# Attention: joining of blocks in four parts, scalings over three steps, z turned behind the fourth transposes, late matmuls of odd steps in the products' bank

## The chip, the cores and the metric

The kernel runs on one core of one Trainium2 chip. The time is the device time of that core in microseconds, the median of three runs. The engines of a core work in parallel, each through its own queue of instructions in program order, and wait for each other by semaphores: TensorE (PE; its weight loads are PEld), VectorE (DVE), ScalarE (ACT), GpSimd (POOL) and SyncE (SP, which issues the DMAs).

## The reference

The program is one layer of three parts, in 32-bit floats:

```
x = x + cross_attention(layernorm(x), ctx)      # x: 16 x 128 x 512, ctx: 16 x 2048 x 512, 16 heads of 32
x = x + mamba_and_mlp(layernorm(x))             # selective scan over 128 steps, then a gelu MLP with two rmsnorms
x = x + mixture_ffn(layernorm(x))               # shared and expert product, two best of 7 gates
```

What the change touches is the attention:

```
attn = softmax(q @ k.T * scale)                 # over 2048 context rows, for each head
out  = (attn @ v) reshaped to 128 x 512
x    = x + out @ wo.T + bo
```

The kernel takes the 2048 context rows in four blocks of 512, each with its own maximum and its own sum of exponentials. The four blocks of a head are joined afterwards: with m the maximum over the blocks, each block's product is multiplied by exp(m_block - m) over the sum of (block sum x exp(m_block - m)).

## The kernel before

The first phase is one long loop over steps u = 0 to 255 (`live`), step u = 16 b + 4 sb + hg: batch b of 16, context block sb of 4, group hg of four heads. A tail of steps up to 313 runs the rest of the scans, interleaved with the MLP and the last part. Each step is written out by hand, and each engine runs it in the order of the code. TensorE, in a live step: the scores of four heads (`scores`, line 299, into the four PSUM banks `bank0` to `bank3`), the product of the step before with v (`weighted`, L343, into `avp`), the first half of a Strassen-like product that makes k and v of the next block (`x_products`, L237, in the PSUM tiles `pa` and `pc`), the transposes of the exponentials (`turn`, L330: four groups of four, group i in a bank), the "late" matmuls, and the second half of the products (`y_products`, L237). One step of two has one product in that second half (odd u, `pa` only), the other has two (even u, `pc` and `pa`).

VectorE takes the maxima of the four banks (L307), ScalarE the exponentials (L317) and copies of transposed banks (L335); one of the four is copied by VectorE (L333). From step 54 on, the scans of the second part run beside this (LAG = 22 steps behind the end of a pair of batches): in every step ScalarE makes decays (L656), VectorE two scans (L670) and products (L673), GpSimd the inputs (L635) and the running sums (L682, L686); every fourth step (u = 1 mod 4) GpSimd ends a group with L689, L690 and L691. GpSimd also makes the sums t of context tiles (L229) in these steps.

The work that comes once per batch is put into tables by step: `loads` (at the step's start), `head` (ahead of the maxima), `middle` and `late` (behind the third or fourth group of transposes; `late` functions get a bank), `behind` (behind the late ones, into `pc`), `after`, and `inner` (at the end, ahead of `y_products`' sums). With e = 16 (b + 1), the step behind the batch's last, these are:

- `joined`, `shares`, `joined_second`, `joined_third`: the joining factors (L418 four copies that gather the maxima, L423 their least negative, L424 the differences, L428 the exponential on ScalarE, L432 to L434 the sum and its reciprocal, L439 the factors).
- `spread_out` (L445, GpSimd, spreads a block's factors over 512 columns in a tile `fx`) and `scaled` (four transposes L451 of `fx`, and VectorE's multiply, L456 for block 0 and L458 for the others; for these GpSimd adds the result into `aT`, L459).
- `attended` in step e+6: the output projection (`out_proj`, L464) of `aT`, and the addition to x.
- `normed` and `z_turned` (L511, copy L513): the layernorm of the second part and its transposes, in steps e+7 and e+8.
- For the next batch: `load_x`, `moments_of`, `root_of`, `normal` (L373, and L376 on GpSimd), `turned` (L385, copied by L387) and `queries` (L395).

A step with late work does three groups of transposes, then the late matmuls in banks 3, 0, 1 and so on, and then the fourth group in the next bank. A bank can be used again when the copy or multiply that reads it is done; the scores of the next step need all four.

Of the kernel before, what the change touches and what calls it, by code (L numbers as in the profile page):

```python
# [34 lines left out]
def perceiver_layer(ctx: ExitStack, tc: tile.TileContext, a: dict, out: bass.AP):  # L35
# [73 lines left out]
    with ExitStack() as es:  # L109
# [251 lines left out]
        def moments_of(b):  # L361
            moments(keep, mv[:, b, :], xts[b])
            xts[b, "r"] = root_first(keep, mv[:, b, 1:2], 1e-5)

        def root_of(b):
            root_second(*xts[b, "r"])
# [15 lines left out]
        def turned(b, ps):  # L382
            xn = xts.pop((b, "n"))
            for kc in range(KC):
                nc.tensor.transpose(heads(ps)[:, kc, :], xn[:, kc * P : (kc + 1) * P], ident)  # L385
            xnT = keep.tile([P, KC, P], FP, tag="fx", name="xnT")
            nc.vector.tensor_copy(xnT, heads(ps))  # L387
            xts[b, "t"] = xnT
# [24 lines left out]
        def joined(b):  # L413

            parts, sm = stats[b]
            nm = keep.tile([P, SB, H], FP, tag="nm", name=f"nm{b}")
            for j in range(4):
                nc.vector.tensor_copy(  # L418
                    nm.rearrange("p s (k j) -> p s k j", j=4)[:, :, :, j], parts[j]
                )  # L420
            lo = keep.tile([P, 1, H], FP, tag="lo", name="lo")
            flat = lo.rearrange("p a h -> p (a h)")
            nc.vector.tensor_reduce(flat, nm.rearrange("p s h -> p h s"), AX.X, ALU.min)  # L423
            nc.vector.tensor_tensor(nm, lo.to_broadcast([P, SB, H]), nm, ALU.subtract)  # L424
            stats[b] = nm, sm, lo, flat

        def shares(b):
            nc.scalar.activation(stats[b][0], stats[b][0], AF.Exp)  # L428
# [322 lines left out]
        def bank():  # L751
            return free_banks.pop(0)
# [316 lines left out]


        late, after, inner, middle, loads, head, behind = ({} for _ in range(7))

        def put(where, u, f):
            where.setdefault(u, []).append(f)

        for b in range(B):
            s = 16 * b
            if b:
                put(loads, s - 8, lambda b=b: load_x(b))
                put(loads, s - 5, lambda b=b: load_w(0, b))  # L1080
                put(inner, s - 7, lambda b=b: moments_of(b))
                put(middle, s - 6, lambda b=b: root_of(b))
                put(inner, s - 6, lambda b=b: normal(b))
                put(late, s - 5, lambda ps, b=b: turned(b, ps))
                put(late, s - 4, lambda ps, b=b: queries(b, ps))
            e = s + 16
            put(loads, e + 5, lambda b=b: load_w(3, b))
            put(inner, e - 1, lambda b=b: joined(b))
            put(middle, e, lambda b=b: shares(b))
            put(head, e + 1, lambda b=b: joined_second(b))  # L1090
            put(head, e + 2, lambda b=b: joined_third(b))
            for sb in range(SB):
                put(inner, e + 2 + sb // 2, lambda b=b, sb=sb: spread_out(b, sb))
                put(late, e + 3 + sb // 2, lambda ps, b=b, sb=sb: scaled(b, sb, ps))
            put(late, e + 6, lambda ps, b=b: attended(b, ps))
            put(middle, e + 7, lambda b=b: root_of(b))
            put(inner, e + 7, lambda b=b: normed(b))
            put(late, e + 8, lambda ps, b=b: z_turned(b, ps))
        for g in range(NG):
            p = 32 * (g + 1)  # L1100
            for ec in range(EC):
                put(loads, p + 8 + ec, lambda g=g, ec=ec: load_win(g, ec))
                put(loads, p + 8 + ec, lambda g=g, ec=ec: load_win(g, EC + ec))
                put(late, p + 9 + ec, lambda ps, g=g, ec=ec: x_part(g, ec, ps))
                put(late, p + 9 + ec, lambda ps, g=g, ec=ec: z_part(g, ec, ps))
                put(after, p + 10 + ec, lambda g=g, ec=ec: silu_first(g, ec, xas))
                put(after, p + Z_GATES[ec], lambda g=g, ec=ec: silu_first(g, ec, zss))
            put(late, p + 18, lambda ps, g=g: x_proj(g, ps))
            s = p + LAG
            for ec in range(EC):  # L1110
                put(loads, s - 4 + 4 * ec, lambda ec=ec: load_dtproj(ec))
                put(behind, s - 3 + 4 * ec, lambda ps, g=g, ec=ec: dt_first(g, ec, ps))
                put(middle, s - 2 + 4 * ec, lambda g=g, ec=ec: dt_second(g, ec))
                put(inner, s - 2 + 4 * ec, lambda g=g, ec=ec: dt_third(g, ec))
            for i in range(GB):
                for ec in range(WS):
                    put(loads, s + 32 + 2 * i, lambda g=g, i=i, ec=ec: load_wout(g, i, ec))
                put(loads, s + 31 + 2 * i, lambda b=g * GB + i: reload_x(b))
                put(late, s + 33 + 2 * i, lambda ps, g=g, i=i: projected(g, i, ps))
# [46 lines left out]
        for u in range(last):  # L1166
            live = u < NU
            g, r = divmod(u - 32 - LAG, 32)
            scans = 0 <= g < NG

            made, phase = divmod(u + 3, 4)
            makes = 0 < made < B * SB
            of, phase = ("k", "v")[phase // 2], phase % 2
            load_bc(u + 2 - 32 - LAG, 0)
            if u % 4 == 1 and made + 1 < B * SB:
                load_ctx(made + 1, ("c00", "c10", "c11"))
            if u % 4 == 2 and made + 1 < B * SB:
                load_ctx(made + 1, ("c01",))
            for f in loads.get(u, ()):
                f()  # L1180
            if scans:
                decays(g, r, 0)
            if u > NU:
                while fed < feeds * (u - NU) // (last - 1 - NU):
                    feed(fed)
                    fed += 1
            load_bc(u + 1 - 32 - LAG, DS)
            if u == NU + 1:
                load_rows()
            if live:  # L1190
                scores(u)
            if 1 <= u <= NU:
                weighted(u - 1)
            if u == NU:
                att.close()
                give_back(flat(pa), banks[2], banks[1], flat(avp))
                open_ffn()
            if u == NU + 8:
                load_wex()
            for f in head.get(u, ()):  # L1200
                f()
            if live:
                maxima(u)
            if makes:
                x_products(of, made, phase, pa, pc)
            if live:
                exps(u)
            if makes and u % 4 == 1:
                ctx_sums(made, ("t1", "t2"))
            if 0 <= u + 1 - 32 - LAG < 32 * NG:  # L1210
                inputs(*divmod(u + 1 - 32 - LAG, 32))
            if makes and u % 4 == 1:
                ctx_sums(made, ("t3", "t4"))
            silu_third()
            if scans:
                scan(g, r, 0)
            if makes:
                hold(of, made, pa, "u1")
            if scans:
                decays(g, r, 1)  # L1220
            if makes:
                x_sums(of, made, phase, pa, pc)


            after_turns = late.get(u, ())
            if live:
                for i in range(3 if after_turns else 4):
                    turn(u, i, i)
            if scans:
                scan(g, r, 1)  # L1230
            for f in middle.get(u, ()):
                f()
            for i, f in enumerate(after_turns):
                ps = banks[(3 + i) % 4] if live else bank()
                f(ps)
                if not live:
                    give_back(ps)
            if live and after_turns:
                turn(u, 3, (3 + len(after_turns)) % 4)
            for f in behind.get(u, ()):  # L1240
                ps = flat(pc) if makes else banks[2] if live else bank()
                f(ps)
                if not live:
                    give_back(ps)
            for f in after.get(u, ()):
                f()
            for f in inner.get(u, ()):
                f()
            if makes:
                y_products(of, made, phase, pa, pc)  # L1250
                y_sums(of, made, phase, pa, pc)
            silu_second()
# [76 lines left out]
```

## Time and profile before

| what | us |
|---|---|
| median of 3 runs (3818.95 to 3823.20) | 3820.44 |
| the profiled execution, its own time | 3821.1 |
| its span in the trace | 3819.3 |
| steps u = 0 to 255 begin and end at about | 57.6 and 3126 |
| TensorE busy in the span | 3747.7 |
| VectorE busy | 2711.8 |
| ScalarE busy | 2445.3 |
| GpSimd busy | 2104.1 |

The span is the time from the first to the last instruction of the program in the trace. Rows of a group give the line, engine, operation, tiles and shapes, the count, the busy time, the mean duration and the idle time of the engine in front. Rows in order of time give the start, the duration and what is merged in them; times such as "+5.64" in the text are counted from the start of the step's first score matmul. The granted TensorE clock is 0.993 of full.

### The profile page before, as it was taken

The page shows a single profiled execution, that of the slowest core. Times are in us where ns is not written, and L with a number is a line of the kernel's source. Part 1 is how long each engine was busy: PE and PEld are TensorE (multiplying, and loading weights), DVE is VectorE, ACT ScalarE, POOL GpSimd, SP SyncE. Part 2 cuts the span into 40 slices and gives each one's busy share as a digit, 9 for nine tenths or more (in the row PEclk, how much of TensorE's full clock was granted, in tenths as well). Part 3 has the DMA queues.
Part 4 walks back from the last instruction along what each step waited for, and adds up shares of the span by engine and source line. Part 5 has one row for each costly group of instructions (what it writes and reads, how often), then busy time and mean ns, then how long its engine had stood idle before and what let it go on. Part 6 is the DMA issues. An engine that isn't in the chain of part 4 may idle for free.

```text
span 3819.3 us, 70341 instructions
## 1 busy us (share of the span) xinstructions
PE 3747.7 (98%) x26120; PEld 2856.3 (75%) x26120; DVE 2711.8 (71%) x4852; ACT 2445.3 (64%) x5847; POOL 2104.1 (55%) x1968
## 2 busy tenths in 40 slices
PE   7999999999999999999999999999999989999999
PEld 6878787778777877788778877787878766656555
DVE  3444444887878787878788778877887777677843
ACT  3555556777767776777677767776777665545421
POOL 1111113676657666765666666666675667567730
PEclk9999999999999999999999999999999999999999
DMA  3111122444353435343534453445444447577752
GB/s 92 39 38 42 45 75 65 145 141 155 121 172 133 158 119 182 130 155 115 188 125 147 129 191 123 145 131 179 135 157 131 158 169 272 193 263 257 264 191 72
DMA packets 341223, 548.40 MB, mean 144 GB/s; under 512 B 24432, under 2 KB 225408, under 8 KB 340624
## 3 DMA queue, kind: packets, MB, share of 16 engines
q1 hardware_dynamic: 340464, 543.28, 42.9%
q8 instruction: 206, 3.38, 0.3%
q14 instruction: 137, 1.12, 0.1%
q0 software_dynamic: 416, 0.63, 0.1%
HBM read 527.29 MB, written 16.52 MB: 142 GB/s over the span
## 4 chain that ended last, share of the span: by engine, by line
PE 84%; DVE 9%; ACT 3%; issue 2%; DMA 1%; POOL 1%; SPq 0%; DVEq 0%; ACTq 0%; POOLq 0%
PE pa L237 21%; PE pc L237 15%; PE bank L330 10%; PE bank L299 7%; PE avp L343 6%; PE bank L518 5%; PE bank L865 3%; PE bank L699 3%; DVE hst L670 2%; PE bank L834 2%; PE bank L960 2%; DVE nm L307 2%; PE bank L395 2%; DVE w L673 2%; PE bank L464 1%
## 5 line engine op out<-in xcount | busy, mean ns | idle before, releaser
L307 DVE TENSOR_REDUCE nm<-bank 128x1 f32<-128x512 f32 x1024 | 634.6, 681 | 251.1 <-PE bank L299 250.2
L686 POOL TENSOR_TENSOR ysum<-ysum,w 128x512 f32<-128x512 f32 x384 | 500.5, 1303 | 483.4 <-DVE hst L649 303.0
L317 ACT ACTIVATE pr<-bank,nm 128x512 f32<-128x512 f32 x1024 | 689.7, 687 | 94.6 <-DVE nm L307 89.1
L635 POOL TENSOR_TENSOR w<-dx,bc 128x512 f32<-128x512 f32 x512 | 649.7, 1290 | 3.8
L335 ACT COPY pT<-bank 128x512 f32<-128x512 f32 x816 | 437.8, 585 | 222.3 <-PE bank L330 218.1
L670 DVE TENSOR_TENSOR_SCAN hst<-hst,w 128x512 f32<-128x512 f32 x456 | 556.9, 1221 | 12.3 <-ACT hst L656 8.5
L330 PE MATMUL bank<-ident,pr 128*128 128x128 f32 x4096 | 525.8, 275 | 16.4 <-ACT pr L317 14.5
L656 ACT ACTIVATE hst<-dt,alog 128x254 f32<-128x254 f32 x912 | 436.5, 479 | 147.3 <-DVE hst L649 128.7
L330 PEld LDWEIGHTS bank<-ident,pr 128*128 128x128 f32 x4096 | 472.7, 142 | 74.7 <-ACT pr L317 22.3
L343 PEld LDWEIGHTS avp<-pT,v 128*32 128x32 f32 x8192 | 208.0, 109 | 193.7 <-issue 193.7
L673 DVE TENSOR_TENSOR w<-hst,bc 128x512 f32<-128x512 f32 x456 | 315.1, 691 | 23.7 <-DMA bc<-bcd 8.3
L299 PE MATMUL bank<-kt,qT 32*128 32x512 f32 x2048 | 297.2, 640 | 6.1 <-DVE avs L458 5.6
L229 POOL TENSOR_TENSOR t<-c,c 128x512 f32<-128x512 f32 x128 | 164.4, 1284 | 251.6 <-PE pc L237 244.4
L343 PE MATMUL avp<-pT,v 128*32 128x128 f32 x8192 | 276.7, 276 | 0.0
L237 PE MATMUL pa<-t,ks 128*128 128x256 f32 x1024 | 248.7, 386 | 0.0
L237 PE MATMUL pa<-vs,t 128*128 128x256 f32 x1008 | 244.7, 386 | 0.0
L518 PE MATMUL bank<-zT,win 128*128 128x256 f32 x968 | 222.0, 383 | 4.6 <-ACT hs L848 4.6
L237 PEld LDWEIGHTS pa<-vs,t 128*128 128x128 f32 x1008 | 185.4, 190 | 34.7 <-issue 10.1
L317 ACT ACTIVATION_READ_ACCUMULATOR pr<-bank,nm 128x1 f32 x1024 | 209.5, 205 | 0.0
L237 PEld LDWEIGHTS pa<-t,ks 128*128 128x128 f32 x1024 | 184.7, 190 | 32.6 <-issue 10.5
L333 DVE COPY pT<-bank 128x512 f32<-128x512 f32 x208 | 143.8, 691 | 89.3 <-PE bank L330 87.8
L518 PEld LDWEIGHTS bank<-zT,win 128*128 128x128 f32 x968 | 181.5, 192 | 28.7 <-ACT hs L848 5.0
(301 smaller groups left out, 6849.8 us busy)
## 6 DMA issues: line engine op xcount, KB each, us to landing
bc<-bcd SPq DMA_DIRECT2D x512, 512.0 KB, 4.3
c<-in_ctxT_dram SPq DMA_DIRECT2D x256, 256.0 KB, 4.2
wf<-in_w_dram SPq DMA_DIRECT2D x128, 512.0 KB, 7.1
wqo<-in_wqkvo_dram SPq DMA_DIRECT2D x128, 256.0 KB, 4.8
win<-in_win_dram SPq DMA_DIRECT2D x128, 256.0 KB, 4.5
wout<-in_wout_dram SPq DMA_DIRECT2D x128, 256.0 KB, 4.0
x<-in_x_dram SPq DMA_DIRECT2D x16, 256.0 KB, 3.7
x1d<-x SPq DMA_DIRECT2D x16, 256.0 KB, 2.2
```

Of the source, the lines that this page charges most:

```text
L237: nc.tensor.matmul(ps[:, r, :], l[:, kc, r * P : (r + 1) * P], m[:, kc, :], start=(i in (1, 2, 5) and r == 0 and kc == 0), stop=(r == 1 an ...
L299: nc.tensor.matmul(banks[j], qts[b][rows, hg, :], kts[u // 4, hg][rows, :], start=True, stop=True)
L307: nc.vector.tensor_reduce(stats[b][0][j][:, sb, hg : hg + 1], banks[j], AX.X, ALU.max, negate=True)
L317: nc.scalar.activation(pr[:, j, :], banks[j], AF.Exp, bias=nm[j][:, sb, hg : hg + 1], accum_out=sm[:, sb, h : h + 1],)
L330: nc.tensor.transpose(ps[:, j, :], prs[u][:, j, i * P : (i + 1) * P], ident)
L335: nc.scalar.copy(pT, ps)
L343: nc.tensor.matmul(avp[j * HD : (j + 1) * HD, hg, :], vts[u // 4, hg // 2, i // 2][:, i % 2, hg % 2 * P + j * HD : hg % 2 * P + (j + 1) * HD],
L518: nc.tensor.matmul(ps, w[:, kc, :], zTs[g][:, kc, :], start=(kc == 0), stop=(kc == KC - 1))
L635: nc.gpsimd.tensor_tensor(w, dx.unsqueeze(1).to_broadcast([P, NH // 2, GT]), bcs[g * 32 + r, 0][:, i * NH // 2 : (i + 1) * NH // 2, :], AL ...
L656: nc.scalar.activation(bt(h[:, k, :])[:, :, 1:], bt(dt)[:, :, 1:], AF.Exp, scale=aneg[:, ec, n : n + 1],)
L670: nc.vector.tensor_tensor_scan(flat, flat, w.rearrange("p n t -> p (n t)"), 0.0, ALU.mult, ALU.add)
L686: nc.gpsimd.tensor_tensor(s, s, w, ALU.add)
```

## The change

The joining of a batch's four blocks, before in three functions (`joined`, `joined_second`, `joined_third`), gets a fourth: the four copies stay in `joined`, the reduction and the differences become `joined_first`. The copies move from the end of step e-1 to the head of step e, `joined_first` to the end of step e, the exponential (`shares`) from e to e+1, and `joined_second` from the head of step e+1 to its end. `joined_third` stays.

The four scalings move from two in step e+3 and two in e+4 to one in e+3, two in e+4 and one in e+5, and the spreading in front of them from e+2 and e+3 to e+2, e+3 and e+4.

The next batch's moments, root, normalisation and transposes come one step earlier each; its load and its queries stay.

In steps e+8 all four groups of transposes come first, and the turned z behind them in bank 0 (`brief`). In odd steps with products the last late function gets the bank of `pc`, unless a `behind` function uses it in that step. The count of transposes in front of late work and the bank of the last group are otherwise as before.

```diff
@@ joined
                 nc.vector.tensor_copy(
                     nm.rearrange("p s (k j) -> p s k j", j=4)[:, :, :, j], parts[j]
                 )
+            stats[b] = nm, sm
+
+        def joined_first(b):
+            nm, sm = stats[b]
             lo = keep.tile([P, 1, H], FP, tag="lo", name="lo")
             flat = lo.rearrange("p a h -> p (a h)")
             nc.vector.tensor_reduce(flat, nm.rearrange("p s h -> p h s"), AX.X, ALU.min)
@@ the tables
-                put(inner, s - 7, lambda b=b: moments_of(b))
-                put(middle, s - 6, lambda b=b: root_of(b))
-                put(inner, s - 6, lambda b=b: normal(b))
-                put(late, s - 5, lambda ps, b=b: turned(b, ps))
+                put(inner, s - 8, lambda b=b: moments_of(b))
+                put(middle, s - 7, lambda b=b: root_of(b))
+                put(inner, s - 7, lambda b=b: normal(b))
+                put(late, s - 6, lambda ps, b=b: turned(b, ps))
                 put(late, s - 4, lambda ps, b=b: queries(b, ps))
             e = s + 16
             put(loads, e + 5, lambda b=b: load_w(3, b))
-            put(inner, e - 1, lambda b=b: joined(b))
-            put(middle, e, lambda b=b: shares(b))
-            put(head, e + 1, lambda b=b: joined_second(b))
+            put(head, e, lambda b=b: joined(b))
+            put(inner, e, lambda b=b: joined_first(b))
+            put(middle, e + 1, lambda b=b: shares(b))
+            put(inner, e + 1, lambda b=b: joined_second(b))
             put(head, e + 2, lambda b=b: joined_third(b))
             for sb in range(SB):
-                put(inner, e + 2 + sb // 2, lambda b=b, sb=sb: spread_out(b, sb))
-                put(late, e + 3 + sb // 2, lambda ps, b=b, sb=sb: scaled(b, sb, ps))
+                put(inner, e + 2 + (sb + 1) // 2, lambda b=b, sb=sb: spread_out(b, sb))
+                put(late, e + 3 + (sb + 1) // 2, lambda ps, b=b, sb=sb: scaled(b, sb, ps))
...
             put(late, e + 8, lambda ps, b=b: z_turned(b, ps))
+            brief.add(e + 8)
@@ the step
             after_turns = late.get(u, ())
+            first = not after_turns or u in brief
             if live:
-                for i in range(3 if after_turns else 4):
+                for i in range(4 if first else 3):
                     turn(u, i, i)
...
+            n = len(after_turns)
             for i, f in enumerate(after_turns):
-                ps = banks[(3 + i) % 4] if live else bank()
+                if not live:
+                    ps = bank()
+                elif u % 2 and makes and i == n - 1 and u not in behind:
+                    ps = flat(pc)
+                else:
+                    ps = banks[(3 + i + first) % 4]
                 f(ps)
                 if not live:
                     give_back(ps)
-            if live and after_turns:
-                turn(u, 3, (3 + len(after_turns)) % 4)
+            if live and not first:
+                turn(u, 3, (3 + n) % 4)
```

More of the change, by code (lines that the diff above doesn't have):

```diff
@@ L1071, in perceiver_layer @@
         late, after, inner, middle, loads, head, behind = ({} for _ in range(7))
+        brief = set()
         def put(where, u, f):
```

## The prediction

> **What bounds the kernel now.** I read the page first: busy time and the chain that ended last.
>
> ```profile
> PE 3747.7 (98%) x26120; PEld 2856.3 (75%) x26120; DVE 2711.8 (71%) x4852; ACT 2445.3 (64%) x5847; POOL 2104.1 (55%) x1968
> PE 84%; DVE 9%; ACT 3%; issue 2%; DMA 1%; POOL 1%; SPq 0%; DVEq 0%; ACTq 0%; POOLq 0%
> ```
>
> TensorE sets the time: 98% busy, 84% of the chain. The matmuls stay the same, so the change can only remove or add gaps between them. The waits of TensorE show how little there is to remove:
>
> ```profile
> PE bank L330 <- ACT pr L317: 14.5, 23, 6.5
> PE bank L299 <- DVE avs L458: 5.6, 12, 0.5
> ```
>
> Columns are total us, times, longest. The first includes one wait of 6.5 us at the end of the attention; the second is 12 waits of 0.47 us, one per batch with scans running (b = 3 to 14). Then I measured each step, from its first score matmul (L299) to the next step's. A step repeats with period 32 to 0.02 us: 9.21 us odd and 10.94 even, plus 0.43 or 0.44 per group of four transposes or dt product, 3.45 for an x/z pair, 3.43 for the output projection. What exceeds that sum is stall. I write e = 16(b+1); the example is b = 7, e = 128, which starts at 1554.84.
>
> **The step that decides.** The fourth scaling moves from step e+4 to e+5, one step ahead of the projection in e+6, which multiplies the aT that GpSimd sums at L459. Busy times by window for steps 133 and 134:
>
> ```profile
> 1609.97:1619.18 9.21, 9.21 (x82) 7.30 (x81) 8.12 (x13) 7.44 (x18) 8.90 (x9) 1.00 0.58 188
> 1619.18:1633.55 14.37, 14.37 (x98) 10.29 (x97) 11.73 (x22) 8.87 (x21) 13.98 (x14) 1.00 0.38 135
> ```
>
> The columns are length, then PE, PEld, DVE, ACT, POOL busy. GpSimd averages 55% but here works 8.90 of 9.21 and 13.98 of 14.37 us: it has a backlog. In order of time (start, us), GpSimd and then TensorE:
>
> ```profile
> 1609.26 2.69 POOL L459 TENSOR_TENSOR aT<-aT,avs 128x512 f32<-128x512 f32 x2
> ...
> 1622.41 2.63 POOL L686 TENSOR_TENSOR ysum<-ysum,w 128x512 f32<-128x512 f32 x2
> 1625.11 0.73 POOL L689 TENSOR_TENSOR ysum<-ysum 128x256 f32<-128x256 f32 x1
> 1625.92 0.73 POOL L690 TENSOR_TENSOR ysum<-ysum,xa 128x256 f32<-128x256 f32 x1
> 1626.73 0.73 POOL L691 TENSOR_TENSOR zs<-ysum,zs 128x256 f32<-128x256 f32 x1
> ```
>
> ```profile
> 1626.12 3.60 PE L464 MATMUL bank<-wqo,aT 128*128 128x512 f32 x8
> ```
>
> Today both last sums are done at 1611.95, 14 us before L464. In the new program the third sum takes the second's place there, and the fourth is issued in step e+5 behind that step's scans, so behind L691: e+5 is 1 mod 4, where a scan closes its group with L689 to L691. Step 133's GpSimd work runs without idle from 1609.26 to the end of L691 at 1627.46. Two instructions join it: the fourth spreading (L445, median 0.61), now issued behind the two sums of e+4 instead of in e+3, and the sum itself (1.27). It lands at 1627.46 + 0.61 + 1.27 = 1629.34. TensorE reaches the projection at 1626.12 + 0.44 = 1626.56, as step 133 grows by four transposes. The 0.39 us wait of step 132 (below) shifts GpSimd by 0.39 and the step end by 0.28, 0.11 more lateness. GpSimd's end to a TensorE start took 0.18 where L572 waits for L566 (1784.39 to 1784.57). The wait is 2.78 + 0.11 + about 0.1 = **3.0 us**. Behind it on TensorE stand the fourth turn, both late products and the next scores, so all of it is time. The trace shows no L464 wait of this kind; its bounds are 2.6 (spans on GpSimd are rough) and 3.4 (each sum at its slowest, and the wake-up in full). Position of L691 against the step is equal to 0.04 us in steps 70 to 246, so 12 times: 12 x 3.0 = **+36.0 us**. For b = 0 to 2 GpSimd has no scans yet and is idle by +1.2 us of step e+6, or earlier; for b = 15 L691 ends at 3182.98 and L464 starts at 3187.5: no wait.
>
> **Joining in parts.** Step 128 is 11.94 against 10.94:
>
> ```profile
> 1555.34 1.46 DVE L418 COPY nm<-nm 128x16 f32<-128x16 f32 x4
> 1556.83 0.26 DVE L423 TENSOR_REDUCE lo<-nm 128x16 f32<-128x64 f32 x1
> 1557.13 0.88 DVE L424 TENSOR_TENSOR nm<-lo,nm 128x64 f32<-128x64 f32 x1
> 1557.93 2.47 DVE L307 TENSOR_REDUCE nm<-bank 128x1 f32<-128x512 f32 x4
> ```
>
> The copies stay ahead of the maxima (now as "head"), L423 and L424 go behind the transposes. Maxima start 1.13 us earlier, at +1.96. Step 136 starts them at +1.70, and there the exponentials, held by the copy of avp, end at +5.49, before the transposes at +5.64; at +1.96 the same copy holds them. I take 0.95 saved, 0.05 left for the late value sum: six steps (64 to 224), **-5.7**. In the other parity (80 to 240) step 144 exceeds its sum by 0.17: its copies ran in idle time at the end of 143 and now stand behind L561 in 144, beside L635.
>
> [...] L418 alone takes 0.17 in idle, 1.02 beside L686; L424 0.22 or 0.88; L432 0.21 or 1.29. By idle rows the maxima of 144 would start near +1.85 and the six steps gain 1.0[...]. I take 0. The later joining operations stand where VectorE has idle time; the worst, the multiply and two small ones at the end of e+1 and L439 at the head of e+2, start the maxima of step 130 at +1.75 instead of +1.16, inside the 0.97 us between last exponential (+4.67) and transposes (+5.64). Without that cover: 0.6 each. The exponential of shares (0.28) lies in ScalarE's idle end of step e+1.
>
> **Three scaling steps.** Step 131 ends in the 0.47 us wait: bank 0's multiply (L458) is the second of two. With one scaling it is L456 in bank 3, to +10.43 of a step that is now 10.08 long. That is the case of step 155/156, where one transposed block in bank 3 (L387, ending equally at +10.43) holds the fourth head's scores 0.39 us. New: 10.08 + (10.94 + 0.87 + 0.39 + 0.04) + 9.65 = 31.97, old 11.08 + 11.96 + 9.21 = 32.25: 12 x -0.28 = **-3.4**. In e+5 the late transposes use pc: its last reader L257 ends at +6.80, they start at +6.95, cost 0. In bank 3 they would hold the next scores about 0.8.
>
> **Normalisation a step earlier.** The turned block leaves steps 155 and 139 for 154 and 138. The 0.39 wait of 156 goes. But in steps 2 mod 4 ScalarE runs L664 before its copies:
>
> ```profile
> 1674.38 0.49 ACT L664 ACTIVATE xa<-xa,dskip 128x256 f32<-128x256 f32 x1
> 1674.78 1.05 ACT L335 COPY pT<-bank 128x512 f32<-128x512 f32 x2
> ```
>
> Bank 0 is free at +7.62 there (+7.24 in odd steps); the next user comes at +7.39 and waits 0.29. So six times -0.10 and six times +0.29: **-0.6 and +1.7**. SyncE's order does not change: x is loaded in the same step, has landed 4.1 us into it at the latest (step 120), and the moments now read it past +10 of that step. Moments, root and normalisation lie in idle time of VectorE and ScalarE at the ends of steps e+8 and e+9; L376 moves a step up GpSimd's queue, ahead of products (L635) that are used a step later.
>
> **z behind the fourth transposes, other pc uses.** In step 136 both z and the fourth turn need bank 0's copy in either order (7.77, wait to 7.83): 0. The x/z and projected products in pc are read before the next step's products at +3.91: 0.
>
> **Sum.** +36.0 - 5.7 - 3.4 - 0.6 + 1.7 = **+28.0 us**. The profiled execution took 3821.1 (span 3819.3, 1.8 around it), so 3849.1; on the median 3820.44, which is 0.7 lower, **3848.4**. The rest of the program I leave at 0, within -2 and +4 for the tail.
>
> **Rivals.** (1) The sum is not late. If GpSimd's queue in e+5 ran 3 us shorter, only the gains stand: 3820.44 - 8.0, with one more in the other joining steps, 3811.4. For it: spans on GpSimd are rough and it idles 45% overall. Against: 8.90 of 9.21 busy in that very step. It decides when the wait falls below 8.0/12 = 0.67 us; 0.10. (2) Half the wait, 1.5 us: 18.0 - 8.0, 3830; if GpSimd's chain tightens. Nothing in its gaps of 0.08 us allows it; 0.07. (3) A second new wait: the spreading pushes L229's sum t toward its product in step 134 (ends +1.37 now, about +1.6, read at +2.08), and the joining gains vanish[...]: 12 x 0.3 + 5.7 more, 3858; 0.09. (0) My forecast, 0.74, own range 3838 to 3857.
>
> **Chances and range.** 0.2% (7.6 us) is about what a measurement can tell from no change. Rival 1 lies at its edge: 0.07 faster, 0.03 same; with small remainders faster 0.08, same 0.05, slower 0.87. The range 3838 to 3859 holds cases 0 and 3 and leaves out 1 and 2.
>
> **What would show it.** Right: TensorE's waits list L464 for POOL aT L459, 12 times near 3.0; steps 70 to 246 near 17.4 instead of 14.37; the L458 wait gone, a 0.39 wait at step 132; step 128 near 11.0. Wrong: L459 three times early and no such wait, or a step 128 that stays at 11.9.

## The result and the profile after

The changed kernel took 3866.87 us (median of four runs, 3858.64 to 3871.27); the kernel before, with a fourth run added, 3821.82. The ratio is 1.0116, with an interval of 1.0104 to 1.0128: slower by some 45 us. The forecast was 3848.4, with a range of 3838 to 3859. Direction and place were right; the loss is 18 us larger than forecast and lies above the range.

The profiled execution of the changed kernel, the slowest of its four, took 3871.3 (span 3869.5), that of before 3821.1 (span 3819.3). The two spans differ by 50.2 us, and this is what the steps below have to add up to. Behind the joining code the changed file is four lines longer: L459, L464 and L691 of before are L463, L468 and L695 now.

The page of the changed kernel, busy times and the chain that ended last by engine:

```profile
PE 3769.8 (97%) x26120; PEld 2864.5 (74%) x26120; DVE 2695.0 (70%) x4852; ACT 2448.4 (63%) x5847; POOL 2106.8 (54%) x1968
PE 84%; DVE 8%; ACT 3%; POOL 3%; issue 1%; DMA 1%; SPq 0%; DVEq 0%; ACTq 0%
```

TensorE executes the same 26120 matmuls, yet it is busy for 22.1 us longer (3769.8 against 3747.7). A wait alone doesn't make an engine busier; this is the first sign of the part that the forecast left out. GpSimd's share of the chain went from 1% to 3%. TensorE's waits after (total us, times, longest):

```profile
PE bank L468 <- POOL aT L463: 30.5, 12, 2.6
PE bank L330 <- ACT pr L317: 12.2, 18, 5.9
```

The wait that the forecast named is there, 12 times, 2.54 each. The wait of the scores for L458 (12 x 0.47) is gone. GpSimd, and then TensorE, in the steps 133 and 134 (step 134 starts at 1636.07):

```profile
1642.10 0.74 POOL L693 TENSOR_TENSOR ysum<-ysum 128x256 f32<-128x256 f32 x1
1642.92 0.73 POOL L694 TENSOR_TENSOR ysum<-ysum,xa 128x256 f32<-128x256 f32 x1
1643.72 0.73 POOL L695 TENSOR_TENSOR zs<-ysum,zs 128x256 f32<-128x256 f32 x1
1644.40 1.26 POOL L463 TENSOR_TENSOR aT<-aT,avs 128x512 f32<-128x512 f32 x1
```

```profile
1641.70 1.47 PE L330 MATMUL bank<-ident,pr 128*128 128x128 f32 x12
1645.72 5.20 PE L468 MATMUL bank<-wqo,aT 128*128 128x512 f32 x8 [2.55 <-POOL aT L463]
```

The fourth sum stands right behind the group's end, L695, and the projection starts 0.06 us after the sum. But the eight matmuls of the projection, which took 3.60 before, take 5.20 here, and 5.2 to 5.4 in nine of the twelve cases. The granted clock shows why. Behind this gap the trace has it at 0.50 for 3.41 us, from 1645.36 to 1648.77. These rows are that stretch and its two neighbours of the same length, and the gap (1643.17 to 1645.72) lies across the first edge (length, then PE, PEld, DVE, ACT, POOL busy, the granted clock, DMA share and rate):

```profile
1641.95:1645.36 3.41, 1.23 (x12) 0.99 (x10) 2.98 (x5) 2.19 (x5) 3.17 (x5) 1.00 0.10 41
1645.36:1648.77 3.41, 3.05 (x4) 1.50 (x5) 0.47 (x2) 0.00 (x0) 3.41 (x4) 0.50 0.00 0
1648.77:1652.19 3.42, 3.42 (x14) 2.05 (x14) 1.20 (x2) 0.80 (x2) 3.07 (x3) 1.00 0.00 0
```

In the first stretch TensorE works for only 1.23 us. The second runs at half the clock, from 0.36 us before the restart to 3.05 behind it, and the third at the full clock again. Step 118 has the same gap (1453.07 to 1455.60), but in the two stretches of this length over which it lies TensorE works for 2.27 and 2.03 us, and the clock stays at 1.00:

```profile
1450.80:1454.21 3.41, 2.27 (x17) 1.88 (x15) 2.71 (x6) 2.65 (x6) 3.17 (x4) 1.00 0.35 128
1454.21:1457.63 3.42, 2.03 (x5) 1.06 (x6) 1.48 (x3) 0.00 (x0) 3.42 (x4) 1.00 0.00 0
```

Steps 70 to 246 of kind e+6, 14.37 us before, became 17.16 to 17.18 in three cases (118, 182, 246) and 18.66 to 18.88 in nine. The first is the wait: 2.54 of gap, 0.15 that the projection no longer overlaps with the transposes before it, 0.10 of a slower start. The second is the wait and the slow clock. The whole difference, step by step:

| part | forecast | profiled execution |
|---|---|---|
| wait for the fourth sum | 12 x 3.0 = +36.0 | 12 x 2.80 = +33.6 |
| slow clock behind the wait | not in the sum | nine times 1.5 to 1.7 = +14.7 |
| joining, steps 64 to 224 | -5.7 | 6 x -1.00 = -6.0 |
| joining, other parity and the step after next | 0 | +1.0 and +0.4 |
| scalings, steps e+3 to e+5 | -3.4 | -1.9 |
| normalisation, first parity | +1.7 | 6 x 0.385 = +2.3 |
| normalisation, second parity | -0.6 | 5 x -0.04 = -0.2 |
| normalisation, step 58 to 60 | as the second parity | +2.41 - 0.44 - 0.39 = +1.6 |
| z turned later, use of `pc` | 0 | 0 |
| steps 253 and 254 | 0 | -0.7 |
| start and tail | 0, within -2 and +4 | +1.7 and +3.6 |
| all other steps | 0 | +0.1 |
| sum | +28.0 | +50.2 |

Over all traces of this case the start differs from that of before by -1.6 to +1.7 and the tail by -2.8 to +3.6, whatever was edited; these 5.3 us are not put down to the change.

### The profile page after: what moved, and what is told of

Same layout as the page of the kernel before. It is cut to its first block, busy times and chain, and to the rows that moved or that the text cites. A ratio compares the mean times of both kernels' runs of the same rounds, so it can differ in the third digit from the quotient of the medians.

```text
span 3869.5 us, 70345 instructions
## 1 busy us (share of the span) xinstructions
PE 3769.8 (97%) x26120; PEld 2864.5 (74%) x26120; DVE 2695.0 (70%) x4852; ACT 2448.4 (63%) x5847; POOL 2106.8 (54%) x1968
## 4 chain that ended last, share of the span: by engine, by line
PE 84%; DVE 8%; ACT 3%; POOL 3%; issue 1%; DMA 1%; SPq 0%; DVEq 0%; ACTq 0%
PE pa L237 21%; PE pc L237 15%; PE bank L330 10%; PE bank L299 7%; PE avp L343 5%; PE bank L522 5%; PE bank L869 3%; PE bank L838 2%; PE bank L468 2%; PE bank L964 2%; DVE nm L307 2%; PE bank L395 2%; PE bank L703 1%; DVE hst L674 1%; PE pc L703 1%
## 5 line engine op out<-in xcount | busy, mean ns | idle before, releaser
L639 POOL TENSOR_TENSOR w<-dx,bc 128x512 f32<-128x512 f32 x512 | 651.4, 1294 | 5.3 <-DMA bc<-bcd 0.6
L330 PE MATMUL bank<-ident,pr 128*128 128x128 f32 x4096 | 521.7, 274 | 14.8 <-ACT pr L317 12.2
L522 PE MATMUL bank<-zT,win 128*128 128x256 f32 x840 | 194.9, 384 | 5.4 <-ACT hs L852 4.6
L229 POOL TENSOR_TENSOR t<-c,t 128x512 f32<-128x512 f32 x128 | 163.8, 1280 | 36.1 <-issue 19.2
```

The source lines that it names most:

```text
L330: nc.tensor.transpose(ps[:, j, :], prs[u][:, j, i * P : (i + 1) * P], ident)
L522: nc.tensor.matmul(ps, w[:, kc, :], zTs[g][:, kc, :], start=(kc == 0), stop=(kc == KC - 1))
L639: nc.gpsimd.tensor_tensor(w, dx.unsqueeze(1).to_broadcast([P, NH // 2, GT]), bcs[g * 32 + r, 0][:, i * NH // 2 : (i + 1) * NH // 2, :], AL ...
```

## The experiments

The theory: the fourth sum, queued on GpSimd behind a scan group's end, holds the projection; and the gap which this opens on TensorE is by itself enough to lower its clock. Rivals: other parts of the change lose the time; or the slow projections come from something else at that moment, such as a transfer or the arrival of weights.

**The scalings put back**, everything else changed:

```diff
-put(inner, e + 2 + (sb + 1) // 2, lambda b=b, sb=sb: spread_out(b, sb))
-put(late, e + 3 + (sb + 1) // 2, lambda ps, b=b, sb=sb: scaled(b, sb, ps))
+put(inner, e + 2 + sb // 2, lambda b=b, sb=sb: spread_out(b, sb))
+put(late, e + 3 + sb // 2, lambda ps, b=b, sb=sb: scaled(b, sb, ps))
```

> The changed kernel with the four scalings back in steps e+3 and e+4 (two each); all else of the change stays. Theory A (the late fourth sum makes TensorE wait 12 times 2.8 us, and a lower clock after the wait adds about 1.7 us in most of them): both go, the projection starts at +6.95 again in steps 70 to 246, and what is left is the joining (-6 + 1.4), the earlier normalisation (+2 to +4) and small terms: 3820, within 3815 and 3825. Theory B (other moved parts, such as the bank of the products or the earlier normalisation, carry what the wait of 30.5 us does not explain, some 15 us): at least 3832.

Measured: 3820.23 (3816.63 to 3822.59), ratio 0.9999 (0.9991 to 1.0008). All twelve steps e+6 are back at 14.37, L468 has no line in the waits, and the wait of the scores for L462 (L458 before) is back:

```profile
PE bank L330 <- ACT pr L317: 11.6, 17, 5.9
PE pa L237 <- DMA c<-in_ctxT_dram: 9.6, 1, 9.6
PE bank L299 <- DVE avs L462: 5.6, 12, 0.5
```

The two changed lines carry the whole loss; all other parts together change nothing that can be measured.

**The scalings alone**, in the kernel before (the diff above turned round, with the rule for `pc`):

> The kernel before with one edit: the scalings over three steps, with the last late matmuls of odd steps in the bank of the products. Theory A: waits for aT 12 times about 2.55 us, and 6 to 9 projections at a lower clock, 33.5 + 10 to 15 - 1.8: 3863 to 3869. Theory B: only the waits, 3853 or less.

Measured: 3855.46 (3853.07 to 3857.20), ratio 1.0093 (1.0078 to 1.0108). In between the two: the same wait, but only two slow projections. TensorE's first wait, the step at 3043 in order of time, and windows behind that gap and behind another:

```profile
PE bank L464 <- POOL aT L459: 30.4, 12, 2.5
```

```profile
3042.75 0.60 PE L330 MATMUL bank<-ident,pr 128*128 128x128 f32 x4
3045.87 5.23 PE L464 MATMUL bank<-wqo,aT 128*128 128x512 f32 x8 [2.52 <-POOL aT L459]
```

```profile
3045.90:3047.90 2.00, 2.00 (x3) 0.97 (x4) 0.10 (x2) 0.00 (x0) 2.00 (x2) 0.50 0.00 0
3047.90:3049.90 2.00, 2.00 (x5) 0.89 (x4) 0.00 (x0) 0.00 (x0) 1.92 (x3) 0.73 0.33 94
2247.80:2249.80 2.00, 1.99 (x5) 1.03 (x6) 0.14 (x2) 0.00 (x0) 2.00 (x2) 1.00 0.00 0
```

Ten steps are 17.17 and two 18.58 and 18.68, behind gaps that are equal to 0.03 us. So the wait belongs to the scalings alone; how often the clock falls with it is not a matter of the gap's length only.

**The fourth sum on VectorE**, with the scalings in their three steps:

```diff
-nc.gpsimd.tensor_tensor(avs[b], avs[b], t, ALU.add)
+(nc.vector if sb == 3 else nc.gpsimd).tensor_tensor(avs[b], avs[b], t, ALU.add)
```

> The changed kernel with the fourth block's sum into aT on VectorE, right behind its multiply, instead of on GpSimd behind the scan's sums. Theory A (the place in GpSimd's queue is the whole cause): no wait for aT, steps 70 to 246 back at 14.37, the rest of the change as it is: 3816 to 3821, that is the run with the scalings put back (3820.2) less 1.8. Theory D (the fourth scaling is too late in itself, wherever the sum is made[...]): a wait of over 0.5 us stays in the 12 steps, 3824 or more.

Measured: 3820.08 (3816.02 to 3822.78), ratio 0.9999 (0.9990 to 1.0007). No wait for aT, every step e+6 at 14.37. The scaling itself is not late, its queue is: taking the last of four sums out of GpSimd's order removes the whole loss.

**The wait filled with products.** Three further matmuls ahead of the projection, into the bank that it then overwrites:

```diff
 aT, x = avs.pop(b), xts[b]
+for _ in range(3 if 2 < b < 15 else 0):
+    nc.tensor.matmul(ps, ident, x, start=True, stop=True)
 out_proj(aT, b, ps)
```

A first version had six of them:

> The changed kernel with six more matmuls of 128x512 (0.43 us each, 2.6 us) in front of each of the 12 projections, in the projection's bank, which the projection then overwrites; they stand where TensorE waited, so the sum L463 is as late as before. Theory A[...]: TensorE no longer idles over about 0.2 us there, the granted clock stays 1.0, all 12 steps take about 17.2 us instead of 18.7 in nine of them, total 3851 to 3857. Theory C (the slow projections come from something that lands late, such as the weights wqo, or from GpSimd's work beside them): the projections stay slow, total 3864 to 3870.

It measured 3879.15 (3878.98 to 3879.44). The filler had been sized at half its length: one call with 128x512 f32 operands runs as two matmul records, so six are twelve, and they take 5.3 us instead of 2.6. All twelve steps were 19.52 with the projection at its normal rate, and the granted clock was 0.993 over the span (0.988 in the changed kernel), but the time says nothing on the gap. With three:

> The changed kernel with three further products (the identity against x, 128x512, into the same bank, overwritten by the projection) ahead of the output projection of batches 3 to 14. From the run with six of them, 0.86 us each: three take 2.58 us, which is the length of the gap (2.53 to 2.55). Theory A, the idle time of TensorE makes the slow projections: the work fills the wait, no projection is slow, all twelve steps e+6 are 17.1 to 17.3, time 3849 to 3857. Theory B, the slow projections come from something else that lies at that time (a DMA, the weights' arrival): still nine or so steps at 18.7 or more, 3862 or above.

Measured: 3852.30 (3851.30 to 3852.47), ratio 1.0080 (1.0065 to 1.0095). Step 134 in order of time:

```profile
1636.49 2.74 PE L474 MATMUL bank<-x,ident 128*128 128x512 f32 x6
1639.23 3.70 PE L468 MATMUL bank<-wqo,aT 128*128 128x512 f32 x8
```

All twelve steps are 17.17 to 17.21. With more work on TensorE than the changed kernel, this one is 14.6 us shorter: the price of the slow clock, taken away. The sum still holds the projection (it starts 0.05 to 0.06 behind the sum's end in all twelve), and its operands arrive as before. The rival that something else at that moment slows the projection falls.

**The wait filled with transposes**, 24 of the identity in that place:

```diff
 aT, x = avs.pop(b), xts[b]
+for k in range(24 if 2 < b < 15 else 0):
+    nc.tensor.transpose(heads(ps)[:, k % 4, :], ident, ident)
 out_proj(aT, b, ps)
```

> As the run with six matmuls, but with 24 transposes of 128x128 (0.11 us each, 2.6 us) in the wait. If transposes count as work[...]: 3851 to 3857, steps of 17.2. If they do not[...]: the wait plus the transposes ahead are like idle time, projections at half clock in nine or more of 12, total 3864 to 3873.

Measured: 3852.72 (3851.85 to 3854.28), ratio 1.0088 (1.0071 to 1.0104), all twelve steps 17.17 to 17.19. With transposes in the gap the clock stays up as with products: it is 1.00 from 1636.30 to 1638.90, over the transposes, and from 1638.90 to 1642.60, over the projection:

```profile
1636.24 2.78 PE L474 MATMUL bank<-ident 128*128 128x128 f32 x24
1638.95 3.70 PE L468 MATMUL bank<-wqo,aT 128*128 128x512 f32 x8
```

**Half of the gap**: the same with twelve transposes.

> The changed kernel with twelve transposes of the identity ahead of the output projection of batches 3 to 14: by the run with 24 of them (no gap left) they take about half of the wait, so a gap of 1.2 to 1.3 us stays. If a gap of that length is too short to lower the clock: all twelve steps e+6 are 17.1 to 17.3, 3849 to 3857, as with 24. If any gap over some half microsecond can lower it: several of the twelve steps are at 18 or more, 3858 to 3868.

Measured: 3853.11 (3851.22 to 3856.10), ratio 1.0083 (1.0067 to 1.0100). TensorE around the gap, and the clock in the gap and behind it:

```profile
1637.58 1.47 PE L474 MATMUL bank<-ident 128*128 128x128 f32 x12
1640.30 3.70 PE L468 MATMUL bank<-wqo,aT 128*128 128x512 f32 x8 [1.24 <-POOL aT L463]
```

```profile
1639.10:1640.20 1.10, 0.00 (x0) 0.00 (x0) 1.07 (x2) 0.00 (x0) 1.10 (x2) 1.00 0.00 0
1640.30:1642.30 2.00, 2.00 (x5) 1.04 (x6) 0.10 (x2) 0.00 (x0) 2.00 (x2) 1.00 0.03 8
```

Twelve gaps of 1.23 to 1.27 us, and none lowers the clock; all twelve steps are 17.17 to 17.22. A gap of 2.54 can lower it, one of 1.24 did not.

**The joining alone**, in the kernel before:

```diff
+stats[b] = nm, sm
+def joined_first(b):
+    nm, sm = stats[b]
...
-put(inner, e - 1, lambda b=b: joined(b))
-put(middle, e, lambda b=b: shares(b))
-put(head, e + 1, lambda b=b: joined_second(b))
+put(head, e, lambda b=b: joined(b))
+put(inner, e, lambda b=b: joined_first(b))
+put(middle, e + 1, lambda b=b: shares(b))
+put(inner, e + 1, lambda b=b: joined_second(b))
```

> The kernel before with the joining in four parts alone. From the steps of the changed kernel: six steps 64 to 224 1.0 us shorter each, six steps 80 to 240 0.16 longer, six steps 66 to 226 0.07 longer: -4.6, 3815.5. If the joining brings nothing: 3820.

Measured: 3816.66 (3812.92 to 3821.40), ratio 0.9989 (0.9983 to 0.9996): -4.5. Its steps 64 to 224 are 1.00 shorter, as in the changed kernel, from which these rows of VectorE in step 128 are:

```profile
1573.33 1.46 DVE L418 COPY nm<-nm 128x16 f32<-128x16 f32 x4
1574.70 2.47 DVE L307 TENSOR_REDUCE nm<-bank 128x1 f32<-128x512 f32 x4
...
1582.67 0.25 DVE L427 TENSOR_REDUCE lo<-nm 128x16 f32<-128x64 f32 x1
1582.96 1.00 DVE L428 TENSOR_TENSOR nm<-lo,nm 128x64 f32<-128x64 f32 x1
```

Starting at 1572.83, the maxima begin at +1.87 instead of +3.09, and the reduction and the differences run at +9.84, where they hold nothing.

**The normalisation alone**, in the kernel before: `moments_of`, `root_of`, `normal` and `turned` a step earlier, as in the change.

> The kernel before with the next batch's moments, root, normalisation and transposes one step earlier, and nothing else. From the steps of the changed kernel: +0.39 for each of six batches (steps 74 to 234), -0.04 for five, and +1.6 once at steps 58 to 60: +3.7, 3824. If step 58's 2.4 us come from another part: +2.1.

Measured: 3824.92 (3820.00 to 3829.62), ratio 1.0012 (1.0005 to 1.0018): a small loss of 4, of which the trace shows 3.1 in the steps up to 255. The largest piece of it comes once, in step 58. VectorE and TensorE there, in the changed kernel (the step starts at 702.47):

```profile
703.75 1.63 DVE L373 TENSOR_SCALAR xn<-x,mv,rstd 128x512 f32<-128x512 f32 x1
705.30 0.94 DVE L565 SCALAR_TENSOR_TENSOR sg<-zs,sg 128x256 f32<-128x256 f32 x1
706.17 2.47 DVE L307 TENSOR_REDUCE nm<-bank 128x1 f32<-128x512 f32 x4
```

```profile
710.76 0.60 PE L385 MATMUL bank<-ident,xn 128*128 128x128 f32 x4
712.68 0.66 PE L330 MATMUL bank<-ident,pr 128*128 128x128 f32 x4 [1.32 <-ACT pT L335]
```

Step 57 is 9.21 us long, while step 89, its like a period later, has 16.08. In step 90 L373 ends at +0.75 and the maxima start at +1.16; here L373 ends at +2.91, with L565 behind it, and the maxima start at +3.70, against +2.80 in step 58 of the kernel before. The transposes wait 0.34 twice for exponentials and then 1.32 for the copy of bank 0.

**What is worth keeping.** The joining in parts only where it gains (the parity of steps 64 to 224), and, for the wait which the three scaling steps were able to remove, another cure: the second scan of step e+3 is issued behind the late work, so that the scalings' multiplies come ahead of it on VectorE. The same in step e+11, where the copy of a transposed block held the scores.

```diff
-put(inner, e - 1, lambda b=b: joined(b))
+if e % 32 == 0:
+    put(head, e, lambda b=b: joined(b))
+    put(inner, e, lambda b=b: joined_first(b))
...
-            if scans:
+            behind_late = live and scans and after_turns and u % 16 in (3, 11)
+            if scans and not behind_late:
                 scan(g, r, 1)
...
                 f(ps)
+                if behind_late and i == (len(after_turns) - 1 if u % 16 == 3 else 0):
+                    scan(g, r, 1)
```

> The kernel before with two edits: the joining in parts for every second batch only (e = 0 mod 32), and in steps u = 3 and 11 mod 16 the second scan issued behind the late work (all of it, or the first function), so that VectorE empties bank 0 and 3 before the scan. Expected: -6.0 for the joining, steps 67 to 243 without the 0.57 (-6.8), steps 60 to 220 without the 0.39 (-2.3): 3805 if nothing else waits; if the later scan delays the next step's decays and with them the copies: 3815 or more.

Measured: 3809.43 (3805.16 to 3810.14), ratio 0.9968 (0.9956 to 0.9981), faster than both kernels by a little. Two of the five executions, the profiled one among them, meet the 3805 expected; three lie some 4 us above, and what cost those is not known. VectorE in step 131, which starts at 1581.15:

```profile
1588.90 0.68 DVE L460 TENSOR_TENSOR aT<-avs,bank 128x512 f32<-128x512 f32 x1
1589.50 0.68 DVE L462 TENSOR_TENSOR avs<-avs,bank 128x512 f32<-128x512 f32 x1
1590.10 1.22 DVE L674 TENSOR_TENSOR_SCAN hst<-hst,w 128x512 f32<-128x512 f32 x1
```

The multiplies end at +9.03 instead of +11.03, with the scan behind them. Steps 67 to 243 of this kind are 0.54 shorter each (twelve), 60 to 220 are 0.39 shorter (six), 64 to 224 are 1.00 shorter (six): -14.8, of which step 235 gives back 0.29 and step 80 0.17.

## Why the prediction was wrong

**The step that failed** is the sentence that priced the wait: "12 x 3.0 us = +36.0", with everything behind the wait only pushed back. The projection was taken with its 3.60 us from the profile of before, where TensorE never stands still in these steps. Behind a gap of 2.54 us it took 5.2 to 5.4 in nine of twelve cases. The term that the sum lacked is +14.7 in the profiled execution, and removing it alone gave 14.6 (three products) and 14.2 (24 transposes) between medians; with the changed kernel's four executions 12.6 us apart, so close an agreement is luck, as it is not known how many gaps were hit in the three that were not profiled. 3848.4 and 14.6 would have been 3863, near the 3866.87 measured. Of the profiled execution's excess over the sum, 50.2 - 28.0 = 22.2, the slow clock is 14.7 and start and tail are 5.3; the other terms leave 2.2. The range failed for the same reason: its bounds for the wait, 2.6 and 3.4, covered when the sum lands and not the rate at which TensorE goes on. The profile of before had no gap of this length in the scan steps, and I put the price of a restart at nothing without saying so. But its tail had two, of 3.0 and 2.8 us, and the first reads (in order of time, then the stretch of the clock):

```profile
3332.66 0.59 PE L572 MATMUL bank<-xa,xproj 128*64 128x256 f32 x2
3336.25 1.11 PE L572 MATMUL bank<-xa,xproj 128*64 128x256 f32 x2 [3.00 <-POOL xa L566]
3335.89:3339.31 3.42, 3.06 (x11) 2.31 (x12) 2.06 (x5) 3.35 (x7) 3.34 (x4) 0.50 0.04 10
```

Two matmuls of L572 take 0.59 us ahead of that gap and 1.11 behind it. The price stood in the profile; the forecast didn't use it.

**The wait.** Right in place, cause and count: L463 behind L695, 12 times, and nothing for b = 0 to 2 and 15. Its size was 2.80 in place of 3.0: I had the sum end at +9.83 of step 134, and it ends at +9.59. The forecast added 0.11 for the longer step 132, but the sums start at -0.70 of step 133 in both kernels, so GpSimd moved with the step; and the spreading put what follows it back by some 0.54, not 0.61. L695 therefore ends at +8.38 instead of +8.56, and the sum starts 0.05 before that end. From the sum's end to the projection's start it is 0.05 to 0.06, where I had read 0.18 at L572 and put in about 0.1; in that place the transposes ahead still ran until 1784.64, so the 0.18 was not a wake-up alone.

**The joining.** Right for steps 64 to 224 (-6.0 for -5.7). In the other parity I took 0, an estimate; it was +0.14 to +0.18 a step. In step 144 L565 ends at +1.37, and of the four copies L418 behind it the first took 1.26 us and the other three 0.17 each. That first one ends at +2.56, with GpSimd's L639, which had run beside it, at +2.52; so the maxima start at +2.69, against +2.52 in the kernel before. L639 itself lasted 1.48 there, against 1.27 for the L635 of before in that place.

**The scalings.** Step 131 as forecast (10.08). Step 132 12.35 against my 12.24: of its excess of 0.15 in the kernel before I had let 0.11 go, and it stayed: the eight transposes L455 take 1.19 there, as L451 did before, against 1.06 in step 131. Step 133 is 9.66 to 9.67 for 9.65. Together -0.155 per batch instead of -0.28.

**The normalisation.** The copies of bank 0 behind ScalarE's L668 (L664 before) hold TensorE as forecast, 0.35 to 0.39 for my 0.29. Missed was step 58: I used the repeating steps for it, and 57 is short.

**z and `pc`** cost nothing, as forecast.

**The rivals.** Rival 1 (the sum is not late) is made true by the kernel with the fourth sum on VectorE, and gives 3820, not 3811: its steps up to 255 gain 2.6 where I had 8.0, by the scalings (1.9 instead of 3.4), the joining's other steps (+1.4) and the normalisation (+3.7 instead of +1.1). Rival 2 did not occur. Of rival 3 the loss of the joining's gains did not occur either; its time, 3858, was nearest to the result, for another reason.

## What to carry to other kernels

A wait on the engine that sets the time costs its length (here 12 x 2.80 us), and it can also cost what the engine does at a lower clock behind it (here 1.5 to 1.7 us, nine times). Price both, from gaps of that length anywhere in the profile and the granted clock by windows; here a wait of 2.5 us was enough in 9 cases of 12. An operation that is moved one step later stands behind everything that its queue takes in that step: write down that queue, at the step's own phase, before the move, because an engine that idles 45% overall can be full in just that step (GpSimd in step 133 of the changed kernel: 9.36 of 9.67 us). And where two operations collide in one engine's order, turning them round in place (a scan behind the multiplies) can do what a move to another step was to do, without a new queue.

## What the runs showed of the hardware

Gaps of 2.52 to 2.55 us on TensorE were followed by a granted clock of 0.50 in 9 of 12 cases in the profiled execution of the changed kernel, and in 2 of 12 in that of the kernel with the scalings alone; gaps of 1.23 to 1.27, with twelve transposes in them, in 0 of 12. The eleven steps were 1.4 to 1.7 us longer than those with an equal gap and the full clock.

In the changed kernel's trace the gaps that were hit and those that were spared lie differently. Each of the nine half clocks of the scan steps lasted 3.41 us, and in the 3.41 us ahead of it TensorE was idle for 2.13 to 2.55 us. In stretches of the same length, counted on from these, the three spared gaps leave 1.14 to 1.41 us of idle time in each of two neighbours (the rows of steps 134 and 118 in the first section are one case of each). That the idle time in such a stretch decides it is an estimate from these twelve gaps; as a rule it is not shown. The price fits: half of 3.41 us is 1.71, and six of the nine steps lost 1.70 to 1.71; three, whose slow stretch began 0.34 to 0.40 us before the restart, lost 1.49 to 1.51.

Two limits: idle time is taken from the matmul records, whose ends are modelled; and the twelve gaps lie in the scan steps and say nothing of the tail.

With 24 transposes in the gap, 12 times, no step was slow (17.17 to 17.19), and the clock was 1.00 in the case shown; with three products in it the steps were 17.17 to 17.21. Had the 24 transposes acted on the clock as idle time does, the twelve gaps would be at least as long as in the changed kernel, where nine were hit.
